# A two-layer graph kernel: tiles fetched through DRAM turned in place, with the feature parts of h interleaved

## The chip, the cores and the metric

The kernel runs on one core of one Trainium2 chip. The metric is the device time of one execution, in microseconds (us). The core has five engines that matter here: TensorE (PE, matrix products; PEld is its loading of weights), VectorE (DVE), ScalarE (ACT), GpSimd (POOL) and SyncE (SP), which here issues DMAs. SBUF is the working memory of 128 partitions, PSUM the memory into which PE writes, DRAM the large memory outside.

## The reference

`x` has 128 samples of 128 nodes with 512 features (f32), `adj` is one 128 x 128 matrix of zeros and ones. Two layers follow each other, each added to `x`:

```python
# layer 0
h = jnp.maximum(_layernorm(x), 0.0)
q, k, v = h @ Wq.T, h @ Wk.T, h @ Wv.T            # 512 x 512 each
rel = adjacency.T[None] * (q @ k.transpose)       # 128 x 128 a sample
rel = rel / norm(rel, axis=2)
x = x + rel @ v
# layer 1
h = jnp.maximum(_layernorm(x), 0.0)
q, k, v = h @ Wq + bq, h @ Wk + bk, h @ Wv + bv   # 8 heads of 64
weights = softmax(q k^T / 8 + mask)               # mask: -1e9 where adj == 0
x = x + weights @ v
```

(Shortened; the second layer's products are taken head by head.)

## The kernel before

The 128 samples are worked in 32 groups of four (`G = 4`). A group goes through layer 0, then layer 1; four groups are in flight at once, named by their stage in the lists of steps: `f` and `m` are layer 0 (loading and statistics, then the work), `n` and `l` layer 1 (statistics and turning of h, then the products), `p` and `o` the tail of layer 1. The lists `FIRST`, `SECOND`, `ORDER` and `LAST` write the order of all steps out by hand; a step such as `m.T1` calls method `T` of object `m` with 1. Each engine takes its instructions in that order. `ORDER` runs for groups 2 to 31.

**h and its path.** The products need h turned, features on partitions. `hn(i)` makes the normalized h of two samples on ACT (L308) and sends it to a scratch tensor in DRAM in blocks of 32 nodes (`send_blocks`, ACT's queue). `rd(i)` fetches it back with four DMAs on SP's queue, one for each 32 partitions, into a staging tile `u` (`fetch_blocks`, L192). `T(i)` then turns 32 x 32 blocks on DVE from `u` into a tile of h (L320). That tile is laid out `[128, KD, HF]`: four feature parts of 128, and for each the 256 nodes of two samples one after the other. `half_tile` (L345) takes it from a pool with one buffer for each layer and half; `x11`, `x12`, `x21`, `x22` are its four quarters.

**The products.** Each 512 x 512 product is done by seven block products instead of eight (`Product`, L200; the steps P1 to P7), which need the sums `s` of quarters: `sumA` makes s0 and s1, `sumB` s3 and s2, on DVE. In layer 1, s2 is written over x21. Each step is four matmuls with 256 columns (L224), of which the trace shows two records each. For `G`, `Q` and `K` (`turned` true) h or s is the moving operand and the weights are loaded; for `V` it is the other way round. P1, P2 and P4 read h; P7 reads s2, in layer 1 a quarter of an h tile; P3, P5, P6 read s. `R` (L391) multiplies h, loaded as weights, with `gT`.

**Softmax weights and outputs.** The exponentials `e` go the same way through DRAM (`ex` or `exC`/`exD`, then `wr` and `wt`) to become `wT[128, H, 128]`, read by `A` (L632). The attention output goes through DRAM once more (`oc`, `rdo`), is turned by `ot` into a tile `o` (L657), scaled in place (L662) and added to the output in DRAM by a DMA of POOL's queue (L669). For two samples of the last group (`tw`, `An`, `fin`) PE turns the weights.

**Pools** (buffers): `npool` 4 (hn, e, oT: what is sent), `tpool` 3 (the staging tiles `u` of all three kinds), `wpool` 3 (wT, and at the start three pieces of the second layer's weights), `work` 2 (o), `rpool` 2 (squares of rel and their turned copy, o of the last group, pieces of weights at the start).

Of the kernel before, what the change touches and what calls it, by code (L numbers as in the profile page):

```python
# [9 lines left out]
F32 = mybir.dt.float32  # L10
AF = mybir.ActivationFunctionType
ALU = mybir.AluOpType
# [9 lines left out]
def kernel(  # L22
# [21 lines left out]
    NG = B // G  # L44
    HF = D // 2
    PSUM = bass.MemoryType.PSUM

    const = ctx.enter_context(tc.tile_pool(name="const", bufs=1))
    xpool = ctx.enter_context(tc.tile_pool(name="xpool", bufs=8))
    hpool = ctx.enter_context(tc.tile_pool(name="hpool", bufs=1))  # L50
    ppool = ctx.enter_context(tc.tile_pool(name="ppool", bufs=1))
    rpool = ctx.enter_context(tc.tile_pool(name="rpool", bufs=2))
    npool = ctx.enter_context(tc.tile_pool(name="npool", bufs=4))
    tpool = ctx.enter_context(tc.tile_pool(name="tpool", bufs=3))
    wpool = ctx.enter_context(tc.tile_pool(name="wpool", bufs=3))
# [90 lines left out]
    def load1():  # L146
        for name, w in (("q", wq1), ("k", wk1), ("v1", wv1)):
            wr = w.rearrange("(k p) d -> p k d", p=P)
            nc.gpsimd.dma_start(
                wc[name][:, W11 : W21 + 1].rearrange("p h k d -> p (h k) d"), wr[:, :, 0:HF]  # L150
            )
            nc.gpsimd.dma_start(wc[name][:, W22], wr[:, 2:4, HF:D])
            w12[name] = wpool.tile([P, 2, HF], F32, tag="wT", name=f"w12_{name}")
# [35 lines left out]
        nc.scalar.dma_start(d.rearrange("n p j f -> p n (j f)"), src.rearrange("p n j f -> p n (j f)"))  # L189
        return d  # L190

    def fetch_blocks(d, n: int, name: str):  # L192

        u = tpool.tile([P, n * TB, 8 * BK // n], F32, tag="u", name=f"u_{name}")
        dv = d.rearrange("n (i q) j f -> j q (n i) f", q=BK)
        for j in range(TB):
            nc.sync.dma_start(u[j * BK : (j + 1) * BK], dv[j])
        return u

    class Product:  # L200

# [69 lines left out]
    class Layer:  # L271
        n: int

        def __init__(self, g: int):
            n, self.g = self.n, g
            self.mv = small.tile([P, G, 2], F32, tag=f"mv{n}", bufs=2, name=f"mv{n}_{g}")
            self.rstd = small.tile([P, G], F32, tag=f"rstd{n}", bufs=2, name=f"rstd{n}_{g}")
            self.shift = small.tile([P, G], F32, tag=f"shift{n}", bufs=2, name=f"shift{n}_{g}")
            self.half, self.d, self.u = {}, {}, {}

        def load(self, b):
            if (self.g, b) not in x_tiles:
# [19 lines left out]
        def hn(self, i):  # L302

            n, g = self.n, self.g
            hn = npool.tile([P, 2, TB, KD, BK], F32, tag="e", name=f"hn{n}_{g}_{i}")
            for r in range(2):
                b = 2 * i + r
                nc.scalar.activation(  # L308
                    hn[:, r], x_tiles[g, b].rearrange("p (k j q) -> p j k q", j=TB, q=BK), AF.Relu,
                    bias=self.shift[:, b : b + 1], scale=self.rstd[:, b : b + 1],  # L310
                )
            self.d[i] = send_blocks(hn.rearrange("p n j k q -> p n j (k q)"), 2, f"h{n}_{g}_{i}")

        def rd(self, i):
            self.u[i] = fetch_blocks(self.d.pop(i), 2, f"h{self.n}_{self.g}_{i}")

        def T(self, i):

            half = self.half_tile(i)
            nc.vector.transpose(  # L320
                half.rearrange("p k (t i) -> p t k i", i=BK),
                self.u.pop(i).rearrange("p t (k q) -> p t k q", q=BK),
            )

        def hn_pe(self, i):

# [9 lines left out]
        def turn_pe(self, i):  # L336

            half, hn = self.half_tile(i), self.d.pop(i)
            for r in range(2):
                pt = ps_o.tile([P, KD, P], F32, tag="po", name=f"pt_{2 * i + r}")  # L340
                for k in range(KD):
                    nc.tensor.transpose(pt[:, k, :], hn[:, r, k, :], ident)
                nc.scalar.copy(half[:, :, ts(r, P)], pt)

        def half_tile(self, i):  # L345
            n, g = self.n, self.g
            half = hpool.tile([P, KD, HF], F32, tag=f"h{n}{i}", name=f"h{n}_{g}_{i}")
            self.half[i] = half
            if i == 0:
                self.x11, self.x12 = half[:, 0:2, :], half[:, 2:4, :]  # L350
            else:
                self.x21, self.x22 = half[:, 0:2, :], half[:, 2:4, :]
            return half

        def sumA(self):
# [12 lines left out]
            nc.vector.tensor_tensor(self.s[2], self.x11, self.x21, ALU.subtract)  # L368

        def turned(self, k, b):  # L370
            return self.half[b // 2][:, k, ts(b % 2, P)]

    class Layer0(Layer):
        n = 0
# [64 lines left out]
    class Layer1(Layer):  # L439
        n = 1  # L440

        def start(self):
            g = self.g
            self.qT = ppool.tile([P, NH, G * P], F32, tag="pq", name=f"qT_{g}")
            self.kT = ppool.tile([P, NH, G * P], F32, tag="pk", name=f"kT_{g}")
            self.Q = Product(self, "q", self.qT, True, bq_sb, name=f"pq_{g}")
            self.K = Product(self, "k", self.kT, True, bk_sb, name=f"pk_{g}")
            self.rs, self.wT, self.ps, self.nmax, self.po, self.e = {}, {}, {}, {}, {}, {}
            self.half_s = {}
            self.dw, self.uw, self.total, self.do, self.uo = {}, {}, {}, {}, {}  # L450

        def sto(self, i):

# [51 lines left out]
                "p (n j f) -> p n j f", n=1, j=TB), 1, f"w_{g}_{b}")  # L505

        def wr(self, b):
            self.uw[b] = fetch_blocks(self.dw.pop(b), 1, f"w_{self.g}_{b}")

        def wt(self, b):  # L510
            g = self.g
            self.rs[b] = small.tile([P, H], F32, tag="rs", bufs=8, name=f"rs_{g}_{b}")
            nc.vector.reciprocal(self.rs[b], self.total.pop(b))
            self.wT[b] = wpool.tile([P, H, P], F32, tag="wT", name=f"wT_{g}_{b}")
            nc.vector.transpose(  # L515
                self.wT[b].rearrange("p h (t i) -> p t h i", i=BK),
                self.uw.pop(b).rearrange("p t (h q) -> p t h q", q=BK),
            )


        def ex_h(self, b, r):
# [41 lines left out]

        def tw(self, b):
            g = self.g
            self.wT[b] = wpool.tile([P, H, P], F32, tag="wT", name=f"wT_{g}_{b}")
# [56 lines left out]
        def A(self, i):  # L623
# [15 lines left out]
        def oc(self, i):  # L639
            g = self.g  # L640
            oT = npool.tile([P, 2, TB, NH, BK], F32, tag="e", name=f"oT_{g}_{i}")
            for n in range(2):
                nc.scalar.copy(oT[:, n], self.po.pop(2 * i + n).rearrange("p k (j q) -> p j k q", q=BK))  # L643
            self.do[i] = send_blocks(oT.rearrange("p n j k q -> p n j (k q)"), 2, f"o_{g}_{i}")
# [7 lines left out]
        def ot(self, i, eng=nc.vector):  # L652
            g, u = self.g, self.uo.pop(i)
            for n in range(2):
                b = 2 * i + n
                o = work.tile([P, NH, TB, BK], F32, tag="o", name=f"o_{g}_{b}")
                nc.vector.transpose(  # L657
                    o.rearrange("p k t q -> p t k q"),
                    u[:, n * TB : (n + 1) * TB].rearrange("p t (k q) -> p t k q", q=BK),
                )  # L660
                heads = o.rearrange("p k t q -> p k (t q)").rearrange("p k (r d) -> p k r d", r=2)
                eng.tensor_tensor(  # L662
                    heads, heads,
                    self.rs.pop(b).rearrange("p (r k) -> p k r", r=2)[:, :, :, None].to_broadcast(
                        [P, NH, 2, HD]
                    ),
                    ALU.mult,
                )
                nc.gpsimd.dma_start(out[g * G + b], o.rearrange("p k t q -> p (k t q)"), accum_op=ALU.add)  # L669

# [100 lines left out]
```

## Time and profile before

| what | value |
|---|---|
| median of 3 runs | 2460.96 us (2460.49 to 2461.54) |
| span of the profiled execution | 2460.6 us |
| TensorE clock granted | 0.999 of full speed |
| DMA engines | mean 178 GB/s, 438.18 MB in all |
| d_h<-hn, ACT's queue | 126 issues of 512 KB, 3.8 us to landing |
| u_h<-d_h, SP's queue | 504 issues of 128 KB, 3.7 us to landing |
| T (L320) | 126 x 1243 ns |
| wt's turn (L515) | 126 x 1210 ns |
| ot's turn and scaling (L657, L662) | 124 x 703 ns, 122 x 692 ns |
| hn (L308) and oT (L643) on ACT | 252 x 807 ns, 124 x 581 ns |

The span runs from the first to the last instruction of one execution taken by the profiler; it lies inside the spread of the timed runs. Groups of instructions are named by line, engine, operation and tiles, written then read; `h` in the name of a matmul says that it reads a tile of h. A matmul's mean duration contains the time it takes to pass through the array, which overlaps the next one; the chain of waits shows the pace.

### The profile page before, as it was taken

The page shows a single profiled execution, that of the slowest core. Times are in us where ns is not written, and L with a number is a line of the kernel's source. Part 1 is how long each engine was busy: PE and PEld are TensorE (multiplying, and loading weights), DVE is VectorE, ACT ScalarE, POOL GpSimd, SP SyncE. Part 2 cuts the span into 40 slices and gives each one's busy share as a digit, 9 for nine tenths or more (in the row PEclk, how much of TensorE's full clock was granted, in tenths as well). Part 3 has the DMA queues.
Part 4 walks back from the last instruction along what each step waited for, and adds up shares of the span by engine and source line. Part 5 has one row for each costly group of instructions (what it writes and reads, how often), then busy time and mean ns, then how long its engine had stood idle before and what let it go on. Part 6 is the DMA issues. An engine that isn't in the chain of part 4 may idle for free.

```text
span 2460.6 us, 40193 instructions
## 1 busy us (share of the span) xinstructions
PE 2450.9 (100%) x14432; PEld 2111.5 (86%) x14432; DVE 1755.6 (71%) x2993; ACT 1012.7 (41%) x3248; POOL 376.8 (15%) x693
## 2 busy tenths in 40 slices
PE   9999999999999999999999999999999999999999
PEld 7888888888888888888888888888888888888888
DVE  6667776677767677776777667776767777677767
ACT  3344443444434344343443344443434434344334
POOL 5111111111111111111011111111111111101111
PEclk9999999999999999999999999999999999999999
DMA  5357656676566775566766667766677566776566
GB/s 190 104 157 206 185 165 173 171 204 198 158 177 172 189 214 163 161 182 180 206 177 172 174 171 205 196 161 175 172 189 209 159 168 178 187 205 176 169 159 165
DMA packets 396407, 438.18 MB, mean 178 GB/s; under 512 B 31600, under 2 KB 289008, under 8 KB 396208
## 3 DMA queue, kind: packets, MB, share of 16 engines
q1 hardware_dynamic: 297376, 201.22, 33.1%
q10 hardware_dynamic: 70000, 165.96, 18.3%
q0 software_dynamic: 28832, 68.44, 13.4%
q8 instruction: 114, 1.87, 0.3%
q14 instruction: 85, 0.70, 0.1%
HBM read 204.80 MB, written 230.69 MB: 177 GB/s over the span
## 4 chain that ended last, share of the span: by engine, by line
PE 92%; DVE 3%; DMA 2%; issue 1%; SPq 1%; ACT 0%; POOL 0%; DVEq 0%; ACTq 0%; POOLq 0%
PE pv_x L224 16%; PE pg_x L224 9%; PE pq_x L224 8%; PE pk_x L224 8%; PE pv_z L224 8%; PE pr L391 4%; PE pq_z L224 4%; PE po L632 4%; PE pg_z L224 4%; PE pk_z L224 4%; PE po L431 4%; PE pv_y L224 4%; PE pss L476 3%; PE pso L476 2%; PE pg_y L224 2%; PE pk_y L224 2%
## 5 line engine op out<-in xcount | busy, mean ns | idle before, releaser
L320 DVE STREAM_TRANSPOSE h<-u_h 128x1024 f32<-128x1024 f32 x126 | 156.6, 1243 | 221.1 <-DMA u_h<-d_h 216.4
L224 PE MATMUL pv_x<-wc_v,h 128*128 128x256 f32 x1280 | 305.9, 382 | 0.4 <-DVE v L248 0.2
L224 PEld LDWEIGHTS pv_x<-wc_v,h 128*128 128x128 f32 x1280 | 240.4, 190 | 51.4 <-issue 20.4
L669 POOL DMA_DIRECT2D out_dram<-o x124 | 110.5, 898 | 971.7 <-DVE o L662 927.5
L308 ACT ACTIVATE hn<-xb,shift,rstd 128x512 f32<-128x512 f32 x252 | 191.1, 807 | 149.2 <-POOL shift L300 128.0
L224 PE MATMUL pv_z<-wc_v,s 128*128 128x256 f32 x1024 | 245.1, 382 | 0.0
L224 PEld LDWEIGHTS pv_z<-wc_v,s 128*128 128x128 f32 x1024 | 192.0, 190 | 28.6
L232 ACT COPY gT<-pg_x 128x512 f32<-128x512 f32 x96 | 56.2, 585 | 364.3 <-PE pg_x L224 363.4
L224 PE MATMUL pq_x<-h,wc_q 128*128 128x256 f32 x768 | 181.7, 379 | 0.6 <-DVE h L320 0.5
L224 PE MATMUL pk_x<-h,wc_k 128*128 128x256 f32 x768 | 181.5, 379 | 0.0
L224 PE MATMUL pv_x<-wc_v,s 128*128 128x256 f32 x768 | 181.5, 379 | 0.0
L529 ACT ACTIVATE e<-pso,nmax 128x128 f32<-128x128 f32 x504 | 179.1, 392 | 3.3 <-DVE nmax L549 3.3
L289 DVE BATCH_NORM_STATS2 st<-xb 128x6 f32<-128x512 f32 x256 | 171.4, 670 | 8.5 <-DMA xb<-in_x_dram 8.5
L515 DVE STREAM_TRANSPOSE wT<-u_w 128x1024 f32<-128x1024 f32 x126 | 152.5, 1210 | 32.7 <-DMA u_w<-d_w 28.9
L224 PEld LDWEIGHTS pq_x<-h,wc_q 128*128 128x128 f32 x768 | 145.5, 190 | 21.8 <-PE pv_x L224 1.7
L224 PEld LDWEIGHTS pk_x<-h,wc_k 128*128 128x128 f32 x768 | 145.8, 190 | 20.0 <-issue 0.2
L224 PEld LDWEIGHTS pv_x<-wc_v,s 128*128 128x128 f32 x768 | 145.8, 190 | 19.9
L643 ACT COPY oT<-po 128x512 f32<-128x512 f32 x124 | 72.0, 581 | 206.5 <-PE po L632 204.1
L299 POOL TENSOR_TENSOR rstd<-rstd,mhalf 128x2 f32<-128x2 f32 x128 | 90.8, 709 | 409.6 <-DVE shift L298 409.6
L70 POOL DMA_DIRECT2D xb<-in_x_dram x124 | 68.7, 555 | 442.6 <-DMA out_dram<-xb 293.2
L232 ACT COPY v<-pv_x 128x512 f32<-128x512 f32 x96 | 56.2, 586 | 178.3 <-PE pv_x L224 178.3
L224 PE MATMUL pg_z<-s,wc_a 128*128 128x256 f32 x512 | 121.2, 379 | 1.4 <-DVE s L363 1.4
(154 smaller groups left out, 4905.7 us busy)
## 6 DMA issues: line engine op xcount, KB each, us to landing
d_h<-hn ACTq DMA_DIRECT2D x126, 512.0 KB, 3.8
u_h<-d_h SPq DMA_DIRECT2D x504, 128.0 KB, 3.7
d_w<-e ACTq DMA_DIRECT2D x126, 512.0 KB, 3.3
u_w<-d_w SPq DMA_DIRECT2D x504, 128.0 KB, 3.2
out_dram<-xb SPq DMA_DIRECT2D x126, 256.0 KB, 3.9
xb<-in_x_dram POOLq DMA_DIRECT2D x124, 256.0 KB, 4.7
d_o<-oT ACTq DMA_DIRECT2D x62, 512.0 KB, 2.9
u_o<-d_o SPq DMA_DIRECT2D x248, 128.0 KB, 4.1
```

The costliest lines, as they stand in the source:

```text
L224: nc.tensor.matmul(ps[:, m, :], lhsT=lhsT, rhs=rhs, start=first and m == 0 and k == 0, stop=k == 1, skip_group_check=True,)
L232: nc.scalar.copy(to, ps)
L289: nc.vector.bn_stats(st, x_tiles[g, b])
L308: nc.scalar.activation(hn[:, r], x_tiles[g, b].rearrange("p (k j q) -> p j k q", j=TB, q=BK), AF.Relu, bias=self.shift[:, b : b + 1], scal ...
L320: nc.vector.transpose(half.rearrange("p k (t i) -> p t k i", i=BK), self.u.pop(i).rearrange("p t (k q) -> p t k q", q=BK),)
L391: nc.tensor.matmul(pr[:, b, :], lhsT=self.turned(k, b), rhs=self.gT[k // 2][:, k % 2, ts(b, P)], start=(k == 0), stop=(k == KD - 1),)
L431: nc.tensor.matmul(po, lhsT=self.rel[:, b, :], rhs=self.v[:, b, :], start=True, stop=True)
L476: nc.tensor.matmul(half[r][:, k, :], lhsT=self.qT[rows, k, ts(b, P)], rhs=self.kT[rows, k, ts(b, P)], start=True, stop=True,)
L515: nc.vector.transpose(self.wT[b].rearrange("p h (t i) -> p t h i", i=BK), self.uw.pop(b).rearrange("p t (h q) -> p t h q", q=BK),)
L529: nc.scalar.activation(e[:, :, i, :], sc[:, k, :].rearrange("p (j q) -> p j q", q=BK), AF.Exp, bias=nmax[:, i : i + 1], accum_out=self.tot ...
L632: nc.tensor.matmul(po[r * HD : (r + 1) * HD, k, :], lhsT=self.v[b // 2][:, b % 2, ts(2 * k + r, HD)], rhs=wT[:, r * NH + k, :], start=True ...
L669: nc.gpsimd.dma_start(out[g * G + b], o.rearrange("p k t q -> p (k t q)"), accum_op=ALU.add)
```

## The change

Three things change, and no arithmetic.

First, what is fetched back from DRAM lands in its final tile, and DVE's block turn reads and writes the same elements. `fetch_blocks` gets the tile as an argument, the staging tiles `u` are gone, and the instructions of `T`, `wt` and `ot` stay one for one. In `wt` the weights keep the order of blocks in which they came, `[128, TB, H, BK]`, so `A` reads for each head four runs of 32. Only for the last group, whose weights `An` loads into the array, are they turned into another tile as before.

Second, so that each block is turned within its own place, h gets the layout `[128, HF, KD]`: the four feature parts are interleaved, and the 256 nodes of one part lie four elements (16 bytes) apart. ACT writes hn and oT with that step ahead of the send, the quarters x11 to x22 become views with that step, and every product that reads h reads it so; the s tiles stay packed. `ot` writes its scaled result from the interleaved tile into a packed `o`.

Third, the pools: one pool of five buffers for all h tiles; one of three for everything else that is fetched (wT, uo, and the three pieces of weights at the start); three instead of four for what is sent; `o` moves into `rpool`, whose two buffers it shares with the squares.

```diff
+    NP, TP, HP = 3, 3, 5
...
-    npool = ctx.enter_context(tc.tile_pool(name="npool", bufs=4))
-    tpool = ctx.enter_context(tc.tile_pool(name="tpool", bufs=3))
-    wpool = ctx.enter_context(tc.tile_pool(name="wpool", bufs=3))
+    npool = ctx.enter_context(tc.tile_pool(name="npool", bufs=NP))
+    tpool = ctx.enter_context(tc.tile_pool(name="tpool", bufs=TP))
...
-    def fetch_blocks(d, n: int, name: str):
-        u = tpool.tile([P, n * TB, 8 * BK // n], F32, tag="u", name=f"u_{name}")
+    def fetch_blocks(d, n: int, u):
         dv = d.rearrange("n (i q) j f -> j q (n i) f", q=BK)
         for j in range(TB):
             nc.sync.dma_start(u[j * BK : (j + 1) * BK], dv[j])
-        return u
...
-            hn = npool.tile([P, 2, TB, KD, BK], F32, tag="e", name=f"hn{n}_{g}_{i}")
+            hn = npool.tile([P, 2, TB, BK, KD], F32, tag="e", name=f"hn{n}_{g}_{i}")
...
-                    hn[:, r], x_tiles[g, b].rearrange("p (k j q) -> p j k q", j=TB, q=BK), AF.Relu,
+                    hn[:, r].rearrange("p j q k -> p k j q"),
+                    x_tiles[g, b].rearrange("p (k j q) -> p k j q", j=TB, q=BK), AF.Relu,
...
         def rd(self, i):
-            self.u[i] = fetch_blocks(self.d.pop(i), 2, f"h{self.n}_{self.g}_{i}")
+            half = self.half_tile(i)
+            fetch_blocks(self.d.pop(i), 2, half.rearrange("p (t q) k -> p t (q k)", q=BK))
...
         def T(self, i):
-            half = self.half_tile(i)
-            nc.vector.transpose(
-                half.rearrange("p k (t i) -> p t k i", i=BK),
-                self.u.pop(i).rearrange("p t (k q) -> p t k q", q=BK),
-            )
+            v = self.half[i].rearrange("p (t q) k -> p t k q", q=BK)
+            nc.vector.transpose(v, v)
...
-            half = hpool.tile([P, KD, HF], F32, tag=f"h{n}{i}", name=f"h{n}_{g}_{i}")
+            half = hpool.tile([P, HF, KD], F32, tag="h", bufs=HP, name=f"h{n}_{g}_{i}")
...
+            first, second = (half[:, :, ts(j, 2)].rearrange("p n k -> p k n") for j in range(2))
...
-            return self.half[b // 2][:, k, ts(b % 2, P)]
+            return self.half[b // 2][:, ts(b % 2, P), k]
...
         def wr(self, b):
-            self.uw[b] = fetch_blocks(self.dw.pop(b), 1, f"w_{self.g}_{b}")
+            self.wT[b] = tpool.tile([P, TB, H, BK], F32, tag="t", name=f"wT_{self.g}_{b}")
+            fetch_blocks(self.dw.pop(b), 1, self.wT[b].rearrange("p t h q -> p t (h q)"))
...
+            u = self.wT[b]
+            if g == NG - 1:
+                self.wT[b] = npool.tile([P, H, P], F32, tag="e", name=f"wn_{g}_{b}")
+                nc.vector.transpose(
+                    self.wT[b].rearrange("p h (t i) -> p t h i", i=BK), u
+                )
+            else:
+                v = u.rearrange("p t h q -> p (t h q)")
+                nc.vector.transpose(v, v)
...
-                            lhsT=self.v[b // 2][:, b % 2, ts(2 * k + r, HD)], rhs=wT[:, r * NH + k, :],
+                            lhsT=self.v[b // 2][:, b % 2, ts(2 * k + r, HD)], rhs=wT[:, :, r * NH + k, :],
...
-            oT = npool.tile([P, 2, TB, NH, BK], F32, tag="e", name=f"oT_{g}_{i}")
+            oT = npool.tile([P, 2, TB, BK, NH], F32, tag="e", name=f"oT_{g}_{i}")
...
         def rdo(self, i):
-            self.uo[i] = fetch_blocks(self.do.pop(i), 2, f"o_{self.g}_{i}")
+            self.uo[i] = tpool.tile([P, 2 * P, NH], F32, tag="t", name=f"uo_{self.g}_{i}")
+            fetch_blocks(self.do.pop(i), 2, self.uo[i].rearrange("p (t q) k -> p t (q k)", q=BK))
...
-                o = work.tile([P, NH, TB, BK], F32, tag="o", name=f"o_{g}_{b}")
-                nc.vector.transpose(
-                    o.rearrange("p k t q -> p t k q"),
-                    u[:, n * TB : (n + 1) * TB].rearrange("p t (k q) -> p t k q", q=BK),
-                )
+                o = rpool.tile([P, D], F32, tag="r", name=f"o_{g}_{b}")
+                ub = u[:, ts(n, P)]
+                v = ub.rearrange("p (t q) k -> p t k q", q=BK)
+                nc.vector.transpose(v, v)
```

More of the change, by code (lines that the diff above doesn't have):

```diff
@@ L152, in load1 @@
             nc.gpsimd.dma_start(wc[name][:, W22], wr[:, 2:4, HF:D])
-            w12[name] = wpool.tile([P, 2, HF], F32, tag="wT", name=f"w12_{name}")
+            w12[name] = tpool.tile([P, 2, HF], F32, tag="t", name=f"w12_{name}")
             nc.gpsimd.dma_start(w12[name], wr[:, 0:2, HF:D])
@@ L278, in __init__ @@
             self.shift = small.tile([P, G], F32, tag=f"shift{n}", bufs=2, name=f"shift{n}_{g}")
-            self.half, self.d, self.u = {}, {}, {}
+            self.half, self.d = {}, {}
         def load(self, b):
@@ L308, in hn @@
                 nc.scalar.activation(
-                    hn[:, r], x_tiles[g, b].rearrange("p (k j q) -> p j k q", j=TB, q=BK), AF.Relu,
+                    hn[:, r].rearrange("p j q k -> p k j q"),
+                    x_tiles[g, b].rearrange("p (k j q) -> p k j q", j=TB, q=BK), AF.Relu,
                     bias=self.shift[:, b : b + 1], scale=self.rstd[:, b : b + 1],
                 )
-            self.d[i] = send_blocks(hn.rearrange("p n j k q -> p n j (k q)"), 2, f"h{n}_{g}_{i}")
+            self.d[i] = send_blocks(hn.rearrange("p n j q k -> p n j (q k)"), 2, f"h{n}_{g}_{i}")
         def rd(self, i):
-            self.u[i] = fetch_blocks(self.d.pop(i), 2, f"h{self.n}_{self.g}_{i}")
+            half = self.half_tile(i)
+            fetch_blocks(self.d.pop(i), 2, half.rearrange("p (t q) k -> p t (q k)", q=BK))
         def T(self, i):
-            half = self.half_tile(i)
-            nc.vector.transpose(
-                half.rearrange("p k (t i) -> p t k i", i=BK),
-                self.u.pop(i).rearrange("p t (k q) -> p t k q", q=BK),
-            )
+            v = self.half[i].rearrange("p (t q) k -> p t k q", q=BK)
+            nc.vector.transpose(v, v)
         def hn_pe(self, i):
@@ L342, in turn_pe @@
                     nc.tensor.transpose(pt[:, k, :], hn[:, r, k, :], ident)
-                nc.scalar.copy(half[:, :, ts(r, P)], pt)
+                nc.scalar.copy(half[:, ts(r, P)].rearrange("p n k -> p k n"), pt)
         def half_tile(self, i):
             n, g = self.n, self.g
-            half = hpool.tile([P, KD, HF], F32, tag=f"h{n}{i}", name=f"h{n}_{g}_{i}")
+            half = hpool.tile([P, HF, KD], F32, tag="h", bufs=HP, name=f"h{n}_{g}_{i}")
             self.half[i] = half
+            first, second = (half[:, :, ts(j, 2)].rearrange("p n k -> p k n") for j in range(2))
             if i == 0:
-                self.x11, self.x12 = half[:, 0:2, :], half[:, 2:4, :]
+                self.x11, self.x12 = first, second
             else:
-                self.x21, self.x22 = half[:, 0:2, :], half[:, 2:4, :]
+                self.x21, self.x22 = first, second
             return half
@@ L449, in start @@
             self.half_s = {}
-            self.dw, self.uw, self.total, self.do, self.uo = {}, {}, {}, {}, {}
+            self.dw, self.total, self.do, self.uo = {}, {}, {}, {}
         def sto(self, i):
@@ L513, in wt @@
             nc.vector.reciprocal(self.rs[b], self.total.pop(b))
-            self.wT[b] = wpool.tile([P, H, P], F32, tag="wT", name=f"wT_{g}_{b}")
-            nc.vector.transpose(
-                self.wT[b].rearrange("p h (t i) -> p t h i", i=BK),
-                self.uw.pop(b).rearrange("p t (h q) -> p t h q", q=BK),
-            )
+            u = self.wT[b]
[7 more added lines that the diff above has]
+                nc.vector.transpose(v, v)
         def ex_h(self, b, r):
@@ L565, in tw @@
             g = self.g
-            self.wT[b] = wpool.tile([P, H, P], F32, tag="wT", name=f"wT_{g}_{b}")
+            self.wT[b] = tpool.tile([P, H, P], F32, tag="t", name=f"wT_{g}_{b}")
             for r in range(2):
@@ L640, in oc @@
             g = self.g
-            oT = npool.tile([P, 2, TB, NH, BK], F32, tag="e", name=f"oT_{g}_{i}")
+            oT = npool.tile([P, 2, TB, BK, NH], F32, tag="e", name=f"oT_{g}_{i}")
             for n in range(2):
-                nc.scalar.copy(oT[:, n], self.po.pop(2 * i + n).rearrange("p k (j q) -> p j k q", q=BK))
-            self.do[i] = send_blocks(oT.rearrange("p n j k q -> p n j (k q)"), 2, f"o_{g}_{i}")
+                nc.scalar.copy(
+                    oT[:, n].rearrange("p j q k -> p k j q"),
+                    self.po.pop(2 * i + n).rearrange("p k (j q) -> p k j q", q=BK),
+                )
+            self.do[i] = send_blocks(oT.rearrange("p n j q k -> p n j (q k)"), 2, f"o_{g}_{i}")
         def rdo(self, i):
-            self.uo[i] = fetch_blocks(self.do.pop(i), 2, f"o_{self.g}_{i}")
+            self.uo[i] = tpool.tile([P, 2 * P, NH], F32, tag="t", name=f"uo_{self.g}_{i}")
+            fetch_blocks(self.do.pop(i), 2, self.uo[i].rearrange("p (t q) k -> p t (q k)", q=BK))
         def otL(self, i):
@@ L655, in ot @@
                 b = 2 * i + n
-                o = work.tile([P, NH, TB, BK], F32, tag="o", name=f"o_{g}_{b}")
-                nc.vector.transpose(
-                    o.rearrange("p k t q -> p t k q"),
-                    u[:, n * TB : (n + 1) * TB].rearrange("p t (k q) -> p t k q", q=BK),
-                )
-                heads = o.rearrange("p k t q -> p k (t q)").rearrange("p k (r d) -> p k r d", r=2)
+                o = rpool.tile([P, D], F32, tag="r", name=f"o_{g}_{b}")
+                ub = u[:, ts(n, P)]
+                v = ub.rearrange("p (t q) k -> p t k q", q=BK)
+                nc.vector.transpose(v, v)
                 eng.tensor_tensor(
-                    heads, heads,
+                    o.rearrange("p (k r d) -> p k r d", k=NH, r=2),
+                    ub.rearrange("p (r d) k -> p k r d", r=2),
                     self.rs.pop(b).rearrange("p (r k) -> p k r", r=2)[:, :, :, None].to_broadcast(
@@ L668, in ot @@
                 )
-                nc.gpsimd.dma_start(out[g * G + b], o.rearrange("p k t q -> p (k t q)"), accum_op=ALU.add)
+                nc.gpsimd.dma_start(out[g * G + b], o, accum_op=ALU.add)
     FIRST = """
```

## The prediction

> **What bounds the kernel now.** I read the page's busy shares first, then the chain of waits over one steady group, then the PE groups by operand, and last DVE beside PE where the chain of h meets the matmuls.
>
> The busy shares:
>
> ```profile
> PE 2450.9 (100%) x14432; PEld 2111.5 (86%) x14432; DVE 1755.6 (71%) x2993; ACT 1012.7 (41%) x3248; POOL 376.8 (15%) x693
> ```
>
> PE is never free, so the time falls only if PE gets less to do, and rises with whatever PE does more slowly. The chain (start, length, what) says the same, step after step:
>
> ```profile
> 1203.97 1.73 PE pq_x L224 x8
> ...
> 1217.78 1.73 PE pg_y L224 x8
> ...
> 1233.32 3.57 PE pr L391 x32
> ...
> 2448.32 3.52 PE pn L586 x32
> ```
>
> A product step is four matmuls, recorded as 8, in 1.73 us: 0.216 us a record of 256 columns, 0.84 ns a column. L391 takes 0.112 us for 128 moving columns. L586 has only 64 moving columns but also 128 weight columns and takes 0.110 us: there the load sets the pace, 0.86 ns a column. R starts again every 75.6 us in most groups (1536.01, 1611.61, 1687.20 in the chain); 32 such groups are 2419 of the span's 2460.6, and the other 42 us are the start, the tail and a few late groups. The profiled span is 0.4 us under the median of the runs, 2460.96; I add to the span.
>
> These are the PE groups that read a tile of h (records, then busy us and mean ns of one; busy counts the tails, so I use 0.216 us):
>
> ```profile
> L224 PE MATMUL pq_x<-h,wc_q 128*128 128x256 f32 x768 | 181.7, 379 | 0.6 <-DVE h L320 0.5
> L224 PE MATMUL pk_x<-h,wc_k 128*128 128x256 f32 x768 | 181.5, 379 | 0.0
> L224 PE MATMUL pg_x<-h,wc_a 128*128 128x256 f32 x512 | 121.1, 379 | 0.8 <-DVE gT L248 0.8
> L224 PE MATMUL pg_y<-h,wc_a 128*128 128x256 f32 x256 | 60.5, 379 | 0.0
> L224 PE MATMUL pk_y<-h,wc_k 128*128 128x256 f32 x256 | 60.5, 379 | 0.0
> L224 PE MATMUL pq_y<-h,wc_q 128*128 128x256 f32 x256 | 60.5, 379 | 0.0
> L224 PE MATMUL pv_x<-wc_v,h 128*128 128x256 f32 x1280 | 305.9, 382 | 0.4 <-DVE v L248 0.2
> L224 PE MATMUL pv_y<-wc_v,h 128*128 128x256 f32 x512 | 120.9, 379 | 0.0
> L391 PE MATMUL pr<-gT,h 128*128 128x128 f32 x1024 | 119.5, 275 | 0.0
> ```
>
> In the first six, 2816 records, h moves through the array. In the last three h is the weights: 1792 loads in front of 256 columns, 1024 in front of 128.
>
> **The change, part by part.** No instruction is added or removed on any engine, and their order stays. What moves is where elements lie.
>
> *h interleaved, read by PE.* Each column of h that PE takes now lies 16 bytes from the last one; before, it was the next element. No PE record of this profile reads with such a step, so the price has two ends. Lower end: nothing. The nearest row is DVE's L422, whose 16 inputs lie 16 bytes apart:
>
> ```profile
> L422 DVE TENSOR_REDUCE sums<-part 32x4 f32<-32x16 f32 x128 | 21.7, 170 | 2.4
> L549 DVE TENSOR_REDUCE nmax<-pso 128x4 f32<-128x512 f32 x128 | 88.5, 691 | 4.4
> L493 DVE TENSOR_REDUCE nmax<-pss 128x8 f32<-128x1024 f32 x64 | 78.1, 1220 | 1.1
> ```
>
> The two packed reductions give 1.03 ns an element and 162 ns beside it, so 179 ns for 16 elements; the spread one took 170. DVE shows no price, over 16 elements and at 1.03 ns each. Upper end: a column costs two column times. On L391 the array takes a moving column and a weight column, from two tiles, in the same 0.87 ns; a path that served one lone column at a time would need both times for one. Then 2816 x 0.216 = +608 us. I take this end: PE asks faster than DVE (0.84 against 1.03 ns), on both operands at once, and the row for the lower end is another engine's with 16 elements. A price half way (1.5 times) is +304.
>
> [...]
>
> *h interleaved, loaded as weights.* Lower end nothing, upper end twice 0.110 us a load. In front of 256 columns that is 0.220 against a pace of 0.216: 1792 x 0.004 = 7 us, so the moving pass hides it. On L391 nothing hides it: (0.220 - 0.112) x 1024 = 111 us. Upper end +118; nothing tells the ends apart, so I take half, +59.
>
> *Turn in place (T), sums, ot.* T writes and reads with the 16-byte step, 126 x 1243 ns; ot's two instructions read so (124 x 703, 122 x 692); of the sums, those with h as operand. By L422 this is free; the upper end is another 1.03 ns an element: 1.06 us a T, 0.53 a sum. What covers it is the margin to PE. From DVE's timeline:
>
> ```profile
> 1293.88 1.25 DVE L320 STREAM_TRANSPOSE h<-u_h 128x1024 f32<-128x1024 f32 x1 [3.23 <-DMA u_h<-d_h]
> 1295.16 0.69 DVE L363 TENSOR_TENSOR s<-h 128x512 f32<-128x512 f32 x1
> ```
>
> and PE's:
>
> ```profile
> 1296.67 1.89 PE L224 MATMUL pg_z<-s,wc_a 128*128 128x256 f32 x8
> ```
>
> The sum ends at 1295.85, its reader starts at 1296.67: 0.82 us of cover. In layer 1 the same sum ends at 1272.08 and pq_z starts at 1274.22: 2.14 us. If PE's steps on h double, a group has 19 us more of PE time (88 records x 0.216), and DVE's slack of 20 us a group (75.6 less 54.9 of work) grows with it: zero in my sum.
>
> *hn and oT* are written by ACT with the 16-byte step, 252 x 807 and 124 x 581 ns. ACT is busy 41%; lower end zero, upper end 0.43 us more for each (a doubled element at 0.85 ns, from L163's 1536 elements in 1487 ns and L164's 512 in 620). Zero taken, same cover; two hn lie ahead of each T.
>
> *Fetches.* Their pieces and bytes stay; now each waits for the tile itself instead of a staging tile. With five h tiles, the tile that m.rd0 takes was last read by l.V.P4 one group earlier, m.rd1's and n.rd0's by layer 0's V and R; n.rd1's by l.V.P2, which starts at 1252.88, while that fetch is issued after 1258.63, behind hn1's send. For the shared t tiles the last readers are A0, A1 and ot, each ahead in the order. So SP, on which every later fetch would queue, gets no later release: zero. If one came late by a step, 1.7 us, T1 and its 0.82 us of cover would be next: 0.9 us in 31 groups, 28 us.
>
> *o in the r pool.* Square now takes the buffer of ot1's o, norms the second, so ACT waits for POOL's accumulating DMAs. These are issued at 1307.0 and 1307.9 and land 5.0 us later (median; longest 8.3): 1312.9 at the latest, against square at 1237.65 + 75.6 = 1313.2. Zero; a longest landing holds ACT by 3 us, behind it oc1's copies and, over the norms on DVE, the mask of pso, whose banks O0 needs. O0 starts 1.8 us after they are free, so some 1.2 us in such a group. *Three e tiles for four*: reuse lies three sends back, some 23 us at ten tiles a group, and a send lands in 3.8 us: zero; the same pace of tiles would have to bunch sixfold to matter.
>
> Sum: 2460.6 + 608 + 59 = 3128.
>
> **The rivals.**
>
> *PE reads a spread column at its present rate.* Place: the 2816 records; price zero; it decides if 0.84 ns holds at a 16-byte step. For it: L422, and that PE's pace is the same for weight and moving columns, which looks like a limit of the array and not of the memory. Against it: L422 is small and not PE's. Loads, DVE and ACT free too: 2461, between 2456 and 2466. This is the other side: not slower. A gain over 0.2%, 4.9 us, would have to come out of the 42 us of start, tail and late groups, where nothing is removed.
>
> *PE is free, but the chain of h gets late.* DVE at the upper end: T + sum are 1.59 later against 0.82, 0.77 x 31 = 24 us in layer 0; in layer 1 two T and a sum, 2.65 against 2.14, 0.51 x 32 = 16 us: 2501. With ACT's two writes, 0.86 more in both layers, 2555. It decides from a delay of 0.82 us; L422 speaks against it. Smaller pool waits, up to 28 us, fall in the same band, 2466 to 2560.
>
> *Only the weight load pays:* R takes 3.57 x 2, and the time is at most 2579; 2515 to 2580. For it: L586 shows the load already sets the pace at 128 columns. Against it: moving columns are asked for at the same rate.
>
> **How the numbers follow.** Moving columns pay (with or without loads): 0.48, own range 2765 (half price, no loads) to 3187 (both full). PE free and all hidden: 0.23, of which 0.18 within 0.2% and 0.05 faster by more. Chain late or pool waits: 0.21. Loads alone: 0.08. Slower: 0.48 + 0.21 + 0.08 = 0.77. The 0.2% is about what a measurement of this kernel can tell from no change. The predicted time is the first case's. Since the lower cases hold 0.52, the range must go down to them: from 2459, which takes in most of the no-change case, to 3190; outside lie some 0.1.
>
> **What would show it.** Right: eight records of pq_x<-h take about 3.4 us in the chain where those on s keep 1.73; R takes between 3.57 and 7; a group lasts near 95 us; DVE's share falls below 60%. Wrong: product steps on h keep 1.73 us (then the rivals hold); T near 2.3 us or a wait of pg_z on the sum in every group (second rival); R alone longer (third). A wait of square on out_dram<-o, or of SP on PE ahead of a fetch, would show the pools.

## The result, and the profile after

| | median | spread | ratio to before |
|---|---|---|---|
| before, same chip | 2461.25 us | 2460.49 to 2462.18 | |
| after | 3284.44 us | 3282.26 to 3285.17 | 1.3341, 95% interval [1.3322, 1.3360] |

The change costs 823 us. The profiled execution of after has a span of 3283.4 us at a granted clock of 1.0. Its busy times (busy us, share of the span, instructions):

```profile
PE 3272.8 (100%) x14432; PEld 2374.5 (72%) x14432; DVE 2054.1 (63%) x2993; ACT 1177.8 (36%) x3248; POOL 377.6 (12%) x693
```

PE is still never free, with as many instructions as before. It idles 11 us of the span, where before it idled 10. So PE does not wait longer; it does the same work more slowly. Where, the chain of waits over one group of after says (start, length, what):

```profile
1606.43 3.62 PE pq_x L222 x8
1610.05 1.73 PE pk_z L222 x8
...
1629.73 3.63 PE pg_y L222 x8
1633.36 1.84 PE pv_x L222 x8
...
1649.33 7.36 PE pr L389 x32
1656.68 1.90 PE po L635 x32
...
1685.89 2.18 PE pv_x L222 x8
```

Read the lengths against the 1.73 us of a product step before, and against these three of before's chain:

```profile
1536.01 3.57 PE pr L391 x32
1539.58 1.90 PE po L632 x32
...
1568.24 1.92 PE pv_x L224 x8
```

Three sorts differ. A step with h moving takes 3.62; the next one, on the packed sum s (pk_z), still takes 1.73. A step with h as the weights (pv_x at 1633.36) takes 1.84, others up to 1.87, and the one behind `A` 2.18 for 1.92. R (pr) takes 7.36 for 3.57. `A` (po, L635), which now reads four runs of 32 columns, keeps its 1.90: a run of 32 costs nothing. R starts again after 101.3 us, at 1548.01, 1649.33 and 1750.77.

The extra lengths of one group, times 32 groups, give the whole loss:

| steps on h in a group | longer by, each | x 32 groups |
|---|---|---|
| 11 with h moving | 3.625 - 1.727 = 1.90 us | 668 us |
| R, 32 loads | 7.36 - 3.57 = 3.79 us | 121 us |
| V, 6 of its 7 steps | 0.13 us | 25 us |
| V, the step with 2.18 for 1.92 | 0.26 us | 8 us |
| together | | 822 of 823 us |

The groups of instructions of after (busy us, mean ns of one, idle before them and what ended it) show the same at the loads, and what became of the engines off the path:

```profile
L222 PEld LDWEIGHTS pv_x<-wc_v,h 128*128 128x128 f32 x1280 | 316.8, 326 | 32.4 <-issue 20.6
L389 PEld LDWEIGHTS pr<-gT,h 128*128 128x128 f32 x1024 | 241.4, 328 | 0.8
L306 ACT ACTIVATE hn<-xb,shift,rstd 128x512 f32<-128x512 f32 x252 | 300.7, 1297 | 118.9 <-POOL shift L298 89.7
L320 DVE STREAM_TRANSPOSE h<-h 128x1024 f32<-128x1024 f32 x126 | 258.2, 2049 | 84.6 <-DMA h<-d_h 84.6
L361 DVE TENSOR_TENSOR s<-h 128x512 f32<-128x512 f32 x64 | 68.1, 1065 | 1.1
```

What now reads or writes with the 16-byte step got slower, on PE, DVE and ACT alike: T 2049 ns for 1243, a sum 1065 for some 690, ot's turn 1122 for 703, hn 1297 for 807, oT 1121 for 581. On DVE and ACT it doesn't show in the time, since PE makes up 99% of the chain.

### The profile page after: what moved, and what is told of

It reads as the page before. It is cut to its first block, busy times and chain, and to the rows that moved or that the text cites. A ratio compares the mean times of both kernels' runs of the same rounds, so it can differ in the third digit from the quotient of the medians.

```text
span 3283.4 us, 40890 instructions
## 1 busy us (share of the span) xinstructions
PE 3272.8 (100%) x14432; PEld 2374.5 (72%) x14432; DVE 2054.1 (63%) x2993; ACT 1177.8 (36%) x3248; POOL 377.6 (12%) x693
## 4 chain that ended last, share of the span: by engine, by line
PE 99%; DVE 1%; issue 0%; DMA 0%; ACT 0%; POOL 0%; SPq 0%; DVEq 0%; POOLq 0%; ACTq 0%
PE pv_x L222 14%; PE pq_x L222 12%; PE pk_x L222 12%; PE pg_x L222 10%; PE pr L389 7%; PE pv_z L222 7%; PE po L635 4%; PE pv_y L222 4%; PE pg_y L222 4%; PE pq_y L222 4%; PE pk_y L222 4%; PE pk_z L222 3%; PE pq_z L222 3%; PE pg_z L222 3%; PE po L429 3%; PE pss L474 2%
## 5 line engine op out<-in xcount | busy, mean ns | idle before, releaser
L222 PE MATMUL pq_x<-h,wc_q 128*128 128x256 f32 x768 | 363.8, 630 | 1.6 <-PE pv_x L222 1.4
L222 PE MATMUL pk_x<-h,wc_k 128*128 128x256 f32 x768 | 364.8, 631 | 0.0
L306 ACT ACTIVATE hn<-xb,shift,rstd 128x512 f32<-128x512 f32 x252 | 300.7, 1297 | 118.9 <-POOL shift L298 89.7
L222 PEld LDWEIGHTS pv_x<-wc_v,h 128*128 128x128 f32 x1280 | 316.8, 326 | 32.4 <-issue 20.6
L320 DVE STREAM_TRANSPOSE h<-h 128x1024 f32<-128x1024 f32 x126 | 258.2, 2049 | 84.6 <-DMA h<-d_h 84.6
L222 PE MATMUL pg_x<-h,wc_a 128*128 128x256 f32 x512 | 242.9, 631 | 1.3 <-DVE gT L246 0.8
L389 PEld LDWEIGHTS pr<-gT,h 128*128 128x128 f32 x1024 | 241.4, 328 | 0.8
L389 PE MATMUL pr<-gT,h 128*128 128x128 f32 x1024 | 240.7, 394 | 0.0
L646 ACT COPY oT<-po 128x512 f32<-128x512 f32 x124 | 125.5, 1121 | 180.8 <-PE po L635 180.8
L222 PEld LDWEIGHTS pg_x<-h,wc_a 128*128 128x128 f32 x512 | 105.6, 206 | 111.6 <-issue 108.9
L233 ACT ACTIVATE kT<-pk_x,bk_sb 128x256 f32<-128x256 f32 x192 | 80.5, 470 | 213.5 <-PE pk_x L222 213.5
```

The costliest lines, as they stand in the source:

```text
L222: nc.tensor.matmul(ps[:, m, :], lhsT=lhsT, rhs=rhs, start=first and m == 0 and k == 0, stop=k == 1, skip_group_check=True,)
L233: nc.scalar.activation(to[:, m, :], ps[:, m, :], AF.Identity, bias=self.bias[:, 2 * j + m : 2 * j + m + 1],)
L306: nc.scalar.activation(hn[:, r].rearrange("p j q k -> p k j q"), x_tiles[g, b].rearrange("p (k j q) -> p k j q", j=TB, q=BK), AF.Relu, bia ...
L320: nc.vector.transpose(v, v)
L389: nc.tensor.matmul(pr[:, b, :], lhsT=self.turned(k, b), rhs=self.gT[k // 2][:, k % 2, ts(b, P)], start=(k == 0), stop=(k == KD - 1),)
L646: nc.scalar.copy(oT[:, n].rearrange("p j q k -> p k j q"), self.po.pop(2 * i + n).rearrange("p k (j q) -> p k j q", q=BK),)
```

## The experiments

The theory: interleaving costs PE a price for each column that it finds alone in its 16 bytes, and the rest of the change costs nothing. The rivals: the pools and the in-place turn have a share; the price depends on something other than the 16 bytes; or the chain of h (hn, its send and fetch, T, the sums) is part of the 823 us. "Fake" below is a constant tile that PE reads in place of h, while h is made as ever.

**probe: single instructions with growing steps.** 32 PE records of 256 columns for each float32 step (16 for bfloat16), then loads, DVE, ACT and POOL. A "step" of 4 takes every fourth element.

```diff
+            nc.tensor.matmul(ps[:, 0:256], lhsT=W[:, 0:P], rhs=X[:, 0:256:1], ...)    # step 1; L63: 0:512:2, ...
...
+            nc.tensor.matmul(ps[:, 0:256], lhsT=W[:, 0:P], rhs=R2, ...)               # L76: runs of 2, 32 bytes apart
+            nc.tensor.matmul(ps[:, 0:256], lhsT=WH[:, 0:P], rhs=H[:, 0:256:1], ...)   # L78: bf16
```

> The reference's computation is left out; only single operations with growing steps between elements are run, one after the other. Line theory: every new 16-byte stretch of SBUF costs about 1.78 ns, whatever engine reads or writes it, so an f32 element costs the larger of the engine's own time and 1.78 x step / 4, up to step 4. Then a record of 256 moving columns takes 216 ns packed, 228 at step 2, 341 at step 3, 453 at steps 4, 6, 8 and 16; runs of two columns 32 bytes apart 228; a load of 128 columns 110, 114, 171, 230, and 230 beyond; bf16 moving 107 packed, 114 at step 2, 228 at step 4, 456 at steps 8 and 16; DVE with 512 elements 690 at steps 1 and 2, about 840 at 3, 1070 from 4 on, reading or writing; ACT about 585, 605, 830 and 1120. Rival, a cliff: steps under 16 bytes are free and each engine pays a factor of its own from 16 bytes on; then f32 steps 2 and 3 cost what packed ones cost and bf16 is free up to step 4. Second rival, distance: steps 8 and 16 cost more than step 4. Sixteen elements on 32 partitions at step 4 should take 12 ns more than packed by the first two, although the norms' line of the kernel showed nothing.

The chain of waits of the probe. L61, L63, L65, L67 and L73 have float32 steps of 1, 2, 3, 4 and 16, L76 runs of two elements 32 bytes apart, L78 to L82 bfloat16 steps of 1, 2 and 4:

```profile
69.65 6.91 PE ps L61 x32
76.56 7.25 PE ps L63 x32
83.81 10.88 PE ps L65 x32
94.69 14.44 PE ps L67 x32
...
138.25 13.80 PE ps L73 x32
152.04 7.36 PE ps L76 x32
159.40 1.75 PE ps L78 x16
161.15 1.81 PE ps L80 x16
162.96 3.63 PE ps L82 x16
```

Step 2 costs 5% (7.25 for 6.91), step 3 57%, step 4 doubles the time, and from there on it no longer grows (14.40 and 14.72 us at steps 6 and 8, 13.80 at 16), so distance is not what is paid for. Count the stretches of 16 bytes that 256 columns touch: 128 at step 2, 192 at step 3, 256 from step 4. At 1.77 ns for each (after's 3.62 us / 8 records / 256) that is 227 ns for a record at step 2 (measured 7.25 / 32 = 0.227 us), 340 at step 3 (10.88 / 32 = 0.340) and 453 at step 4 (0.451). The two-element runs (0.230) pay like step 2, and bfloat16 doubles at a step of 4, which is 8 bytes (1.75 to 3.63 us for 16 records), where float32 doubles at 16: a record of packed bfloat16 takes half as long to begin with (0.109 us for 0.216). So in these rows the price follows the count of 16-byte stretches, not a multiple of PE's own column time. DVE and ACT follow (groups; L104, L106 and L110 are a reduction that reads 512 elements with steps 1, 2 and 4, L128 and L130 one of 16 elements with steps 1 and 4, L146 a copy that reads with step 4, L158 one that writes with step 4):

```profile
L104 DVE TENSOR_REDUCE acc<-X 128x1 f32<-128x512 f32 x4 | 2.7, 684 | 0.1
L106 DVE TENSOR_REDUCE acc<-X 128x1 f32<-128x512 f32 x4 | 2.7, 686 | 0.1
...
L110 DVE TENSOR_REDUCE acc<-X 128x1 f32<-128x512 f32 x4 | 4.2, 1048 | 0.1
...
L128 DVE TENSOR_REDUCE acc<-X 32x1 f32<-32x16 f32 x4 | 0.6, 160 | 0.1
L130 DVE TENSOR_REDUCE acc<-X 32x1 f32<-32x16 f32 x4 | 0.7, 168 | 0.1
...
L146 ACT COPY V<-X 128x512 f32<-128x512 f32 x4 | 4.4, 1088 | 0.1
L158 ACT COPY Z<-W 128x512 f32<-128x512 f32 x4 | 4.4, 1094 | 0.1
```

DVE pays nothing at step 2 (686 ns for 684), 20% at step 3 (824 ns) and 53% at 4 (1048 ns). An estimate from these numbers fits: half a stretch is 1.77 / 2 = 0.89 ns, less than DVE's own 1.03 ns an element. At step 4, reading and writing cost the same on ACT (1088 and 1094 ns) and within 2% on DVE (1048 and 1066 ns). And the 16-element reduction, packed, takes 160 ns, not the 179 that the prediction had for it.

**packed_h: the change without the interleaving of h.** The tile of h is packed again, so hn is written packed, and h comes through a staging tile `u` (three buffers of its own) and is turned out of it. The shared pools, the turn in place of wT and uo and the interleaved o stay.

```diff
-            half = hpool.tile([P, HF, KD], F32, tag="h", bufs=HP, ...)
+            half = hpool.tile([P, KD, HF], F32, tag="h", bufs=HP, ...)
...
-            v = self.half[i].rearrange("p (t q) k -> p t k q", q=BK)
-            nc.vector.transpose(v, v)
+            nc.vector.transpose(half.rearrange("p k (t i) -> p t k i", i=BK), self.u.pop(i).rearrange("p t (k q) -> p t k q", q=BK))
```

> The changed kernel with only h packed again (turned out of a staging tile of its own into [128, KD, HF]); the shared h pool of five, the in-place turn of the softmax weights and of the outputs, the pools of three stay. Theory (PE's reads of h are the whole loss): 2461, within 3 us, product steps on h 1.73 us, R 3.57. Rival (part of the 823 us is in the pools, in ACT's and DVE's strided work for the outputs, or in the four runs that A reads): 2470 or more.

2460.52 us (2459.32 to 2461.66), ratio 0.9996 [0.9986, 1.0005]. The pools, the fetch into the final tile for wT and uo, and the interleaved o cost nothing that can be measured. All 823 us come from h: from its layout, or from its direct fetch and its turn in place, which inter_only below takes apart.

**loads_only and moving_only: half of PE's reads each.** On packed_h; in loads_only the loads of R and V read an interleaved fake, in moving_only the moving columns do.

```diff
+    fake = const.tile([P, HF, KD], F32, ...)
+    fakes = [fake[:, :, ts(j, 2)].rearrange("p n k -> p k n") for j in range(2)]
...
+                    if not self.turned and h:      # moving_only: if self.turned and h
+                        xk = fakes[w == W21 or w == T4N][:, k, :]
...
-            return self.half[b // 2][:, k, ts(b % 2, P)]
+            return fake[:, ts(b % 2, P), k]        # loads_only alone
```

> packed_h, but V and R load their weights from a fixed tile of ones that is interleaved as h was, instead of from h (so V, R and all behind them are not the reference's); the moving operands are packed. Theory (PE's price is paid record by record): R +3.79 us and V's seven steps on h +0.13 us each a group, 32 x 4.70 = 150, so 2611. Rival (loads cost only because the strided moving passes hold the memory at the same time): close to 2461.

> packed_h, but the steps on h of G, Q and K take their moving operand from a fixed tile of ones that is interleaved as h was (so gT, qT, kT and all behind them are not the reference's); all loads are packed. Theory: eleven steps a group at 3.625 instead of 1.727 us, 32 x 20.9 = 668, so 3129. Rival (moving and loading interleaved hamper each other, so either alone costs less than its part): under 3080.

loads_only took 2612.67 us, 1.0615 [1.0599, 1.0631]; moving_only 3124.17 us, 1.2693 [1.2672, 1.2715]. The chain of loads_only,

```profile
1604.31 1.73 PE pq_x L229 x8
...
1614.67 1.87 PE pv_x L229 x8
...
1628.78 7.36 PE pr L398 x32
```

and that of moving_only,

```profile
1603.81 3.62 PE pq_x L229 x8
...
1659.06 1.73 PE pv_y L229 x8
1666.13 3.57 PE pr L398 x32
```

take the three numbers of after apart: each kernel has its own half of them and the old pace in the other. With some 151 us for the loads and 662 for the moving columns, 2461 + 151 + 662 = 3274, ten short of after. That leaves no third cause of more than some 10 us, and no sign that the two sorts hamper each other.

**probe_loads: the load by itself.** In the first probe the loads came after the spread bfloat16 reads, when the granted clock had fallen to 0.50 (182 to 195 us), so its packed loads (0.21 us) were no base. Here 64 loads for each step are followed by 128 moving columns (L60: step 1; L66: step 4) or 64 (L72: step 4; L78: step 1); in L80 both operands have step 4, with 256 columns. The clock was 1.00 in all of these stages but L72, where it fell again (0.61).

```diff
+            nc.tensor.matmul(ps[:, ts(i % 4, P)], lhsT=X[:, i % 4 : i % 4 + 509 : 4], rhs=W[:, ts(i % 4, P)], ...)                  # L66
...
+            nc.tensor.matmul(ps[:, ts(i % 2, 256)], lhsT=X[:, i % 4 : i % 4 + 509 : 4], rhs=X[:, i % 4 : i % 4 + 1021 : 4], ...)   # L80
```

> The reference's computation is left out. In the first run of single operations every load took about 0.21 us a record, packed ones too, so something other than the step set their pace; here the place in PSUM rotates and the loaded columns change. Line theory: a load of 128 columns beside 128 moving ones 0.112 us a record at step 1, 0.114 at 2, 0.171 at 3, 0.229 at 4 and 8; beside 64 moving ones 0.110 and 0.229; beside 256 moving ones 0.216 packed and 0.231 at step 4; with one place in PSUM and 64 columns 0.21 again if the place was the cause. Both operands at step 4 and 256 moving columns: 0.45 if the two operands are read side by side, 0.68 if they share one path.

The chain of waits of probe_loads:

```profile
70.33 7.14 PE ps L60 x64
...
96.25 14.93 PE ps L66 x64
...
133.50 14.98 PE ps L72 x64
...
178.46 7.09 PE ps L78 x64
185.55 29.45 PE ps L80 x64
```

A load follows the same curve: 0.112, 0.118, 0.175, 0.233 and 0.238 us at steps 1, 2, 3, 4 and 8, so 1.82 ns a stretch at step 4. A spread load stands at 0.233 us with 128 columns behind it (L66) and at 0.234 with 64 (L72). With both operands spread (L80, both out of one tile) a record takes 0.460 us, hardly more than the 0.451 of its moving columns alone: the load's 0.233 runs beside them, and the two don't add up to 0.68. The place in PSUM, which the expectation suspected, has no part: a packed load takes 0.111 with one place (L78) and with eight (L70). One stage missed its expectation: packed loads with 256 columns (L74) took 0.235 for 0.216; they come right behind L72, and the granted clock from 149 to 163 us was 0.94.

**inter_only: nothing but the layout.** On before, with its pools and staging tiles; T writes an interleaved h out of place.

```diff
-                half.rearrange("p k (t i) -> p t k i", i=BK),
+                half.rearrange("p (t i) k -> p t k i", i=BK),
...
-            half = hpool.tile([P, KD, HF], F32, tag=f"h{n}{i}", ...)
+            half = hpool.tile([P, HF, KD], F32, tag=f"h{n}{i}", ...)
```

> The kernel before with nothing but the tile of h interleaved, by T on its way out of the staging tile; all pools, hn, the softmax weights and the outputs as before. Theory (PE's reads are all of it also in the changed kernel): 2461 + 667 + 121 + 30 = 3279, between 3274 and 3289. Rival (turning in place and the smaller pools add to it): below 3270.

3281.00 us (3280.02 to 3281.99), ratio 1.3325 [1.3306, 1.3345]: after's time to within 4 us, from before's kernel with one layout exchanged. So the layout is the cause, and the direct fetch and the turn in place add nothing to it. Steps of 3.62, 1.84 and R's 7.36 stand in its chain too, and T takes 2027 ns though only its output is spread (in place 2049): the price of reading and that of writing don't add in T.

**pe_packed: the other way round.** The change as it is, but PE reads a packed fake; only the work of SP, ACT and DVE on the interleaved h is left to cost something. PE's steps on h don't wait for the real h here, so what a late T would cost them is not in this run.

```diff
+    fake = const.tile([P, KD, HF], F32, ...)
...
+                    if h:
+                        xk = fake[:, 2 * (w == W21 or w == T4N) + k, :]
...
-            return self.half[b // 2][:, ts(b % 2, P), k]
+            return fake[:, k, ts(b % 2, P)]
```

> The changed kernel, but PE reads h in all products and in R from a fixed packed tile of ones (so everything behind is not the reference's); ACT, DVE, SP and the pools do all of the interleaved work, and the sums s still come from the real tiles. It asks what the rest of the change would cost with PE's reads at their old pace. If the chain of h is late by its measured extra times (hn +0.98, T +0.81, a sum +0.38 us): layer 0 1.35 us beyond its cover of 0.82 in 31 groups, layer 1 0.84 beyond 2.14 in 32, so about 2530, 2500 to 2550. Rival (the other queues absorb it): 2461 to 2470.

2598.63 us (2594.97 to 2608.86), ratio 1.0568 [1.0541, 1.0594]: a miss, some 68 us above what the theory gave. PE's waits in pe_packed (us in all, times, longest):

```profile
PE pq_z L228 <- DVE qT L252: 75.3, 32, 3.7
```

That is three quarters of the idle time, and it is not for the sum s that pq_z reads. Layer 0's wait for a sum, which the expectation had priced at 1.35 us in each of 31 groups, comes to 13.4 us in all (pg_z, 13 times). DVE's timeline in one group of pe_packed says why (start, length):

```profile
1332.93 2.08 DVE L326 STREAM_TRANSPOSE h<-h 128x1024 f32<-128x1024 f32 x1 [2.35 <-DMA h<-d_h]
...
1337.91 2.08 DVE L326 STREAM_TRANSPOSE h<-h 128x1024 f32<-128x1024 f32 x1
...
1341.22 1.08 DVE L367 TENSOR_TENSOR s<-h 128x512 f32<-128x512 f32 x1
1342.34 1.07 DVE L368 TENSOR_TENSOR s<-s,h 128x512 f32<-128x512 f32 x1
1343.33 0.68 DVE L252 TENSOR_TENSOR qT<-pq_y,qT 128x512 f32<-128x512 f32 x1
```

PE's beside it:

```profile
1344.07 1.99 PE L228 MATMUL pq_z<-s,wc_q 128*128 128x256 f32 x8 [2.02 <-DVE qT L252]
```

and the same add before, where pq_z started at 1274.22:

```profile
1272.72 0.69 DVE L248 TENSOR_TENSOR qT<-pq_y,qT 128x512 f32<-128x512 f32 x1
```

DVE adds a finished product to qT, which empties the PSUM bank that pq_z writes next, and this add stands in DVE's order behind both T and the first two sums. From the first T's start (1332.93) to the add's end it is 11.08 us now, 8.62 before: two T at 0.83 more and two sums at 0.40. The first T, behind a longer hn, also starts 0.48 us later against PE's step pq_x. Before, the add ended 0.81 us ahead of pq_z; 2.46 and 0.48 less 0.81 is 2.13, and the pause is 2.02. PE's idle time is 101 us (span 2593.3 less 2492.4 busy) for before's 10, and its busy time is 41 us above before's 2450.9: after some of the pauses the granted clock is lower (0.66 from 1184.5 to 1189.5 in this trace, 1.00 from 1192 on), and two steps there take 2.67 and 2.57 us for 1.73. Together they are the 133 us between the two profiled spans; the medians lie 137 apart.

**pairs: a layout with two parts side by side.** If a stretch costs 1.77 ns, two elements in it nearly hide the price (at PE's own pace they take 2 x 0.84 = 1.68 ns); so h as two pairs of parts, each pair interleaved, still turned in place. It takes two activations for one in hn and eight fetch pieces for four.

```diff
-            half = hpool.tile([P, HF, KD], F32, ...)
+            half = hpool.tile([P, 2, HF, 2], F32, ...)
...
+                for c in range(2):
+                    nc.scalar.activation(hn[:, r, :, c].rearrange("p j q e -> p e j q"), ...)
...
+                for c in range(2):
+                    nc.sync.dma_start(hv[j * BK : (j + 1) * BK, c], dv[j][:, c])
```

> The changed kernel with h interleaved in pairs of parts, 8 bytes between a part's neighbours, still turned in place; the fetch of h takes eight DMAs with pieces of 256 bytes instead of four with 512, and ACT makes hn in four instructions instead of two. Line theory with the measured 0.2266 us a record at step 2: 2816 x 0.0107 = +30, R +2, so 2493, and up to 2510 if the longer hn is late for the sums. [...]

2668.44 us (2661.02 to 2670.16), ratio 1.0832 [1.0815, 1.0849]: a miss by some 160 us. The steps themselves are as expected, 1.81 us with h moving and 3.76 for R; but PE idles 122 us (span 2659.2, busy 2537.0), 80 of them before pq_z for the add of qT. The chain of pairs at such a place:

```profile
1611.27 3.05 DMA d_o<-oT
1614.34 0.30 SPq L320
...
1616.16 2.08 DMA h<-d_h
...
1618.43 1.25 DVE h L325
...
1622.23 0.70 DVE qT L246
1622.97 2.86 PE pq_z L222 x8
1625.83 2.55 PE pq_x L222 x8
```

Here the last of h's pieces go out on SP only when oT's send has landed, though hn's send, issued at 1603.74, had landed 4.2 us after that. The profile puts SP's wait at this line down to oT's send 31 times, 97 us in all; the pieces of h need nothing of oT, and what holds SP there stays open. T (1.25 us, its old length) is late by that, the add of qT too, and PE's next steps run at a granted clock of 0.66 and 0.77. It is the place of pe_packed, reached another way: through a late T1 and not through a longer one.

**pairs_read: the pairs in PE's reading alone.** On packed_h, a fake in the layout of pairs.

```diff
+    fake = const.tile([P, 2, HF, 2], F32, ...)
+    fakes = [fake[:, j].rearrange("p n e -> p e n") for j in range(2)]
...
-            return self.half[b // 2][:, k, ts(b % 2, P)]
+            return fake[:, k // 2, ts(b % 2, P), k % 2]
```

> packed_h, but PE reads h in all products and in R from a fixed tile of ones interleaved in pairs, 8 bytes between a part's neighbours (so all behind them is not the reference's); fetch, hn and T are those of packed_h. It takes the pairs' price for PE by itself, without the longer fetch and hn of the run pairs. Line theory with the rates of the single operations: 2816 x 0.0107 = 30 for the moving columns and 1024 x (0.1184 - 0.1116) = 7 for R's loads, so 2498, between 2493 and 2503. [...] If the 2668 of pairs was PE's reading after all, this run is near 2668.

2494.78 us (2493.86 to 2495.32), ratio 1.0137 [1.0119, 1.0155], as expected. So the reading of pairs costs 34 us, and the other 174 us of pairs come from how h is made and fetched. Whether the longer hn (504 x 607 ns for 252 x 807) or the longer row of fetches on SP (16 issues in 12.82 us where before has 8 in 6.74) does it was not separated. No kernel with h interleaved reaches the time of the kernel before; packed_h, where h is packed, does.

## Why the prediction was right and wrong

The direction, the mechanism and the engine were right: PE bounds the kernel, moving columns of h pay, the steps on s don't, and 3128 was the sum for that case. The measured 3284 lies beyond the range, which ended at 3190. Of the 156 us above the predicted time, 60 are the moving columns and 95 the loads: the mechanism held, and both prices were set too low. By its steps:

- **"Upper end: a column costs two column times"** is the step that failed, for moving columns and for loads. It tied the price to PE's own pace, and 2 x 0.84 ns is no bound. What the runs show is a price of its own, 1.77 ns for each 16-byte stretch: on PE 0.453 us a record, 2.1 times the old one. DVE's 1048 ns in the probe, less the 162 beside its elements, are 1.73 for each of 512. The term was 608 us; in the profile it is 668, in moving_only alone 662.
- **Loads, "I take half, +59"**: 154 us, above even the upper end of 118. Nothing in the trace spoke for half. A load takes 0.230 us and not 0.220; R pays 121 for the 111 of its upper end. The small excess also counts where it was called hidden: a pace of 0.216 hides a load of 0.220 but for 7 us, and doesn't hide 0.230, which costs V 33.
- **The lower end, L422.** "179 ns for 16 elements; the spread one took 170" drew a straight line from 512 and 1024 elements down to 16. In the probe, 16 elements take 160 ns packed and 168 spread. L422's 170 fits the spread value, though it makes four sums of four where the probe makes one of sixteen; so a price of some 8 ns lay in that row unseen, and the line hid it. It fed the first rival, 0.23 of the chances, which the runs exclude.
- **T, sums, ot, hn, oT at zero**: right in the sum, and for the reason given, that DVE's slack grows with PE's time. The upper ends were fair: T 0.81 longer (1.06 taken as the end), a sum 0.38 (0.53), hn 0.49 and oT 0.54 (0.43, too low). DVE's share is 63%, not below 60%, since its 299 us of longer work were left out of that sign.
- **The second rival, 2501 to 2555**, was priced by the cover of the sums, 0.82 and 2.14 us. pe_packed shows 2599. In layer 1 the cover that gives out first is the 0.81 us of qT's add, which no step of the working had looked at, and some pauses cost more than their length, as the clock is lower after them (0.66 in the stretch above). In the changed kernel this is hidden by the slower PE.
- **Pools and fetches at zero**: shown by packed_h for the pools, wT and uo. The direct fetch of h was never tried with packed reads and an unlengthened T; inter_only, which reaches after's time without it, shows that it costs nothing there.

## What to carry to other kernels

Before an operand is interleaved, count the 16-byte stretches that the bound engine must touch, multiply by the 1.77 ns measured here, and compare with that instruction's time; here runs of 32 elements cost nothing (`A`: 1.90 us in both kernels), pairs 5% (1.81 us for a step of 1.73), lone elements 2.1 times (3.62 us). Buy convenience in a layout (an in-place turn, one buffer less) on the side of the engine with slack, never in the operand of the engine that is never free. And where an end of a bound is a multiple, ask what shows that the cost is a multiple at all: one probe, or the nearest row compared at its own size, beats a line drawn through far larger ones.

## What the runs showed of the hardware

- In these stages the price of a spread load didn't follow PE's granted clock. In the first probe the granted clock was 0.60 during the widest bfloat16 reads (167 to 181 us) and 0.50 after them. There loads with a step of 4 took the same 0.233 us as L66 of probe_loads at full clock, while packed ones took 0.21 for 0.11. And in L72 of probe_loads the clock was 0.61 (134 to 148 us), where it was 1.00 in L66 and still in L70 before it, yet its 64 records took 14.98 us, as L66 took 14.93. The first line is the windows view of the probe in the stretch of its packed loads (busy PE, PEld, DVE, ACT, POOL, then the granted clock, DMA share, GB/s), the second that of probe_loads in L72 (without ACT):

```profile
182.00:195.00 13.00, 13.00 (x63) 13.00 (x62) 0.00 (x0) 0.00 (x0) 0.00 (x0) 0.50 0.00 0
```

```profile
134.00:148.00 14.00, 14.00 (x61) 14.00 (x62) 0.00 (x0) 0.00 (x0) 0.61 0.00 0
```

- By the profile PE was at work the whole time in both places, so the lower clock (0.50 and 0.61) came without a pause of PE. Each time spread reads were running, bfloat16 ones in the probe and float32 loads in L72; whether they are the cause was not tried by itself.
- POOL pays less: its addition of 512 elements, with one operand spread, takes 1262 ns packed, 1288 at step 2 and 1512 at steps 4 and 8, 20% more where a reduction on DVE pays 53%.
